# A four-layer graph network: the second product of layer 1 as seven block products, and sums that may stand on either of two engines

## The chip, the core and the metric

The kernel runs on one core of one Trainium2 chip. The core has five engines that run side by side, each with its own queue of instructions in a fixed order: TensorE (PE: matrix products, with PEld for its weight loads), VectorE (DVE), ScalarE (ACT), GpSimd (POOL) and SyncE (SP, which issues transfers). They share the on-chip memory SBUF; products land in PSUM, eight banks of 128 x 512 numbers. An instruction waits until what it needs is there, and everything behind it on its engine waits too.

The metric is the device time of one execution, in microseconds (us).

## What is computed

Input are 128 graphs of 64 nodes with 256 features, float32 throughout, and their adjacency matrices. Four layers follow each other, each as x = layernorm(x + layer(x)):

```python
# layer 0: five steps of a gated update
m = h @ weight[l];  agg = adj^T @ m
r, z = sigmoid(i_r + h_r), sigmoid(i_z + h_z);  n = tanh(i_n + r * h_n)
h = (1 - z) * n + z * h                 # i from agg @ w_ih.T, h_* from h @ w_hh.T
# layer 1
agg = epsilon * x + adjacency @ x
h = silu(rmsnorm(agg @ W1 + b1) * rms_weight)       # 1024 wide
out = h @ W2 + b2                                    # back to 256
# layer 2: log map, adj @ x, exponential map, projection onto the ball
# layer 3: attention with weights exp(e_i + f_j) masked by adj
```

The change is mostly about `h @ W2` in layer 1: per group of graphs a product of 512 x 1024 by 1024 x 256.

## The kernel before

Two graphs make one block of 128 nodes, so that an adjacency block is 128 x 128 with two filled quarters. Four blocks make a group (`NB` = 4, `R` = 512 nodes), and there are 16 groups. `group(g)` (called once per group) records every operation of one group for all four layers; nothing is run while it records. Operations go to one engine (`pe`, `dve`, `act`, `pool`) or are recorded with two possible ones (`flow.either`, used by `copied` and `scaled` for ScalarE or VectorE), each with an assumed duration.

`Flow.issue` then lays the order of all engines. It is a planner, `Plan.advance`: it keeps a clock per engine, looks at the next operations of up to four groups at a time (`WINDOW`), and takes the one that can begin first by the assumed durations; ties are broken by a rank. The rank is one of a few rules (earliest group first, latest group first, or longest remaining path with a lag per group), and `CHOICES` holds a digit for every stretch of `STRETCH` us that says which rule holds there. The string was found by a search. The order so found is fixed: each instruction is tied behind its predecessor on the engine, and only the real waits decide when it runs. Operations flagged `port` are kept from overlapping between VectorE and GpSimd in the plan.

Buffers: a group's tiles live in one of three slots (`s = g % 3`), under tags (`A`, `B`, `U`, `V`, `agg`, `h`, `y`, `hs`, `adjT`); a new tile under a tag waits until all users of the one before are done. The 4-wide tiles of the norms (`tiny`) have two buffers for each name and slot.

The places that matter here, by line of the profile:
- L745 to L749: sums and differences of halves of h or agg, which feed the gates' products. These, and layer 1's first product (L949), are already seven block products in place of eight.
- L762 and L768: the gates' products. Both take 256 columns at a time.
- `state_side`: two quarters of intermediate results in the tile `hs` (L773, L788).
- L884 to L887: the last three steps of the gated update on VectorE.
- L933 and L343: squares of the 1024 hidden features on ScalarE, and their sums (GpSimd, on VectorE in the last two groups). L343 is the helper `pool_sum`, also used to add the biases b2 (`xb`) and W_b (`x_n`).
- L998 and L1000: scaling by the root mean square (VectorE), then silu (ScalarE), for 8 chunks of 128 features. L991, L692 and L1062 are powers of 4 or 8 numbers on GpSimd.
- L313 with `ps_o`: the product with `w2s`, the whole of W2 in SBUF. For every block of 128 nodes 8 chunks of 128 features are multiplied by 256 columns and accumulated:

```python
for k in range(KH):
    pe(256, lambda ps=ps, b=b, j=j, k=k: matmul(
        ps[:, j * D:(j + 1) * D], chunk(k)[0][:, b * P:(b + 1) * P], w2s[:, k, :], k, KH),
        [ps], [*chunk(k)[1], (w2s, k)])
```

- L667, `onto_rows`: the result is added onto the residual on VectorE; in all but the last two groups the same instruction also gives the row's sum for the norm.
- `layer_norm`: the row's sum to a mean (L679), sum of squares on ScalarE (L681), the power on GpSimd (L692), and the scaling (L336 or L337). The last two groups use VectorE's own row statistics (L688, L689).
- L313 also stands for other products (`matmul`): `ps_agg` (aggregation, 128 columns at a time), `ps_sup`, `ps_a`, `ps_att` of layers 2 and 3.

Of the kernel before, what the change touches and what calls it, by code (L numbers as in the profile page):

```python
# [13 lines left out]
AF = mybir.ActivationFunctionType  # L14
# [39 lines left out]
class Plan:  # L54
# [15 lines left out]
    def advance(self, until, rank):  # L70
# [3 lines left out]
        while self.left and clock["PE"] < until:  # L74
            best = None
            for s in range(self.first, min(self.first + flow.WINDOW, len(self.queues))):
                for e, q in self.queues[s].items():
                    opened = False
                    for _, o in zip(range(flow.AHEAD[e]), q):
# [12 lines left out]
                        key = (t + flow.SOONER if len(o.ways) > 1 and e == "DVE" else t, *rank(s, o))  # L92
# [36 lines left out]
class Flow:  # L129
# [16 lines left out]
    SOONER = 0.4  # L146
# [6 lines left out]
    WINDOW, STRETCH, LAGS = 4, 6.0, (0.0, 60.0, 150.0)  # L153
    CHOICES = ("0010000320333333330030000000030000303010330000003330300030300030300003033330301303000001103313000330"
               "0001000001010301301300133000000000300003030301031033030033000000031033031033030300303333030330010330"
               "0000330000300333303103003030300300030130000033000303030000333301300103300003300000003301000033003033"
               "3000000111310003100100311030000003300111101111202220010111101102112122201121121202122111000")
# [81 lines left out]
def kernel(  # L239
# [50 lines left out]
    small = ctx.enter_context(tc.tile_pool(name="small", bufs=2))  # L290
# [51 lines left out]
    def pool_sum(n, o, x0, x1, w, r):  # L342
        pool(0.24 + 0.00211 * n, lambda: nc.gpsimd.tensor_tensor(o(), x0(), x1(), OP.add), w, r)  # L343
# [85 lines left out]
    vecs = unit("hs", S, "vecs", (P, 2, P))  # L429
# [128 lines left out]
    w2s = fixed([P, KH, D], "w2s")  # L558
    flow.op("SP", 0.6, lambda: nc.sync.dma_start(w2s.tile(), w2.rearrange("(k p) d -> p k d", p=P)), [w2s], kb=1024)
# [41 lines left out]
    def group(g):  # L601
# [14 lines left out]
        def tiny(name, shape=(P, NB), dt=F32):  # L616
            t = f"{name}{s}"
            return Buf(lambda: small.tile(list(shape), dt, tag=t, name=f"{name}_{g}"), slot=(t, 2))
# [53 lines left out]
        def layer_norm(y, st, tag, name, norm=None):  # L672
# [4 lines left out]
            m = 2 if norm else 1  # L677
            if summed:
                dve(4, lambda: nc.vector.tensor_scalar(mv[:, :, 0], st[:, :, 0], -1.0 / D, None, OP.mult), [mv], [st])  # L679
                for b in range(NB):  # L680
                    act(400, lambda b=b: nc.scalar.activation(  # L681
                        o[:, b, :], y[:, b, :], AF.Square, bias=mv[:, b, 0:1], accum_out=st[:, b, 1:2]),
                        [(o, b), (st, (1, b))], [(y, b), mv])
                dve(8, lambda: nc.vector.scalar_tensor_tensor(  # L684
                    ve[:, :m, :], over(st[:, :, 1], m), 1.0 / D, eps2[:, :m, :NB], OP.mult, OP.add), [ve], [st])
            else:
                for b in range(NB):
                    dve(256, lambda b=b: nc.vector.bn_stats(st[:, b, :], y[:, b, :]), [(st, b)], [(y, b)])  # L688
# [9 lines left out]
            for b in range(NB):  # L698
                scaled(256, lambda b=b: o[:, b, :], lambda b=b: y[:, b, :], lambda b=b: rstd[:, 0, b:b + 1],
                       lambda b=b: off[:, b:b + 1], [(o, b)], [(y, b), off, rstd], ("DVE",))  # L700
# [21 lines left out]
        def gated(l, h):  # L722
# [20 lines left out]
            def sums(x, i):  # L743
                t = t_of[i]
                dve(R, lambda: nc.vector.tensor_sub(t[:, :2, :], x[:, :, half(1)], halves_of(x[:, 0, :])),  # L745
                    [(t, t1), (t, t3)], [x], True)
                dve(HR, lambda: nc.vector.tensor_sub(t[:, t2, :], x[:, 1, half(1)], t[:, t1, :]),
                    [(t, t2)], [(x, 1), (t, t1)], True)
                dve(HR, lambda: nc.vector.tensor_sub(t[:, t4, :], t[:, t2, :], x[:, 1, half(0)]),  # L749
                    [(t, t4)], [(x, 0), (t, t2)], True)  # L750
# [24 lines left out]
            def state_side():  # L775

                px, py = bank("p_hx"), bank("p_hy")
                hs = u("hs", f"hs{l}", (P, 2, HR))
                su, sv = ((lambda i=i: hs[:, i, :]) for i in range(2))
# [12 lines left out]
                copied(HR, su, lambda: px[:, :HR], [(hs, 0)], [px])  # L792
# [3 lines left out]
                onto(su, px, 1, su, [(hs, 0)], [(hs, 0)])  # L796
                prod(py, 0, w_hn, ms3, sum_of(t3)[1], True)
                onto(sv, py, 0, su, [(hs, 1)], [(hs, 0)])
                prod(py, 1, w_hn, ms1, sum_of(t1)[1])
                prod(py, 0, w_hn, mn22, sum_of(t4)[1])  # L800
                biased(0, 1, py, 0, su, (hs, 0))
                biased(1, 1, py, 1, sv, (hs, 1))
                prod(py, 1, w_hn, ms4, block(1, 1)[1])
                biased(1, 0, py, 1, su, (hs, 0))
# [354 lines left out]
```

## Time and profile before

| what | value |
|---|---|
| median of 3 runs | 2367.19 us (2366.66 to 2367.27) |
| the profiled execution, its time | 2366.68 us |
| its span from first to last instruction | 2364.9 us |
| instructions in the span | 32771 |
| matmul instructions | 11986 |
| read from and written to device memory | 24.69 MB, 8.39 MB |
| granted TensorE clock, mean | 0.994 |

How to read it: the span is cut into busy time per engine; a group of the profile is all instructions of one line, engine, operation and tile, with its count, the time it covers, the mean length of one, and the idle time of the engine just before them with who ended it. The chain of waits goes back from the last instruction to what released each step. A float32 matmul of the code appears as two instructions, each with its own weight load.

### The profile page before, as it was taken

How to read it: one execution, taken by the hardware profiler on the slowest of the kernel's cores; microseconds unless marked ns; L12 is line 12 of the kernel's file. 1: busy time of each engine (PE TensorE's matmuls, PEld its weight loads, DVE VectorE, ACT ScalarE, POOL GpSimd, SP SyncE). 2: the span in 40 equal slices, each digit the busy share in tenths (PEclk: the TensorE clock that was granted, in tenths of full speed). 3: DMA queues.
4: the chain of work that ended last, by engine and by line, in shares of the span. 5: the costliest groups of instructions: out<-in, count | busy, mean ns of one | idle time of the engine just before them, and what ended most of it. 6: DMA issues, size and time to landing. Idle time of an engine off the chain costs nothing.

```text
span 2364.9 us, 32771 instructions
## 1 busy us (share of the span) xinstructions
PE 2329.6 (99%) x11986; PEld 2046.1 (87%) x11986; DVE 1904.2 (81%) x4271; ACT 1236.0 (52%) x2643; POOL 340.1 (14%) x272
## 2 busy tenths in 40 slices
PE   9999999999999999999999999999999999999996
PEld 7888888888888888888888888888888888888874
DVE  5788887887878778787887878787787887788986
ACT  3334555555555555555555555455554555444375
POOL 3102111021010212102021110212102020001021
PEclk9999999999999999999999999999999999999997
DMA  3000000000000000000000000000000000000000
GB/s 123 10 1 12 1 30 1 21 9 1 30 1 27 3 1 30 1 30 1 18 12 1 30 1 27 3 1 30 1 30 1 10 21 1 19 10 1 19 1 27
DMA packets 39440, 35.17 MB, mean 15 GB/s; under 512 B 9924, under 2 KB 38624, under 8 KB 39280
## 3 DMA queue, kind: packets, MB, share of 16 engines
q1 hardware_dynamic: 37552, 31.20, 4.2%
q8 instruction: 95, 1.56, 0.3%
q10 hardware_dynamic: 1328, 1.31, 0.2%
q0 software_dynamic: 400, 0.57, 0.1%
q14 instruction: 65, 0.53, 0.1%
HBM read 24.69 MB, written 8.39 MB: 14 GB/s over the span
## 4 chain that ended last, share of the span: by engine, by line
PE 91%; DVE 7%; ACT 1%; issue 1%; POOL 0%; POOLq 0%; ACTq 0%; DVEq 0%
PE p_r L762 11%; PE p_w L762 11%; PE p_v L762 11%; PE ps_o L313 9%; PE ps_agg L313 7%; PE p_hy L768 6%; PE p_u L762 6%; PE p_iy L768 5%; PE p_hx L768 4%; PE p_ix L768 4%; PE ps_hr L644 3%; PE ps_a L313 2%; PE p_vh L949 2%; PE p_wh L949 2%; PE p_1h L949 2%; PE ps_sup L313 1%
## 5 line engine op out<-in xcount | busy, mean ns | idle before, releaser
L692 POOL TENSOR_TENSOR rstd<-ve,pow 128x4 f32<-128x4 f32 (+1 forms) x64 | 77.7, 1214 | 1319.4 <-DVE ve L684 1213.9
L313 PE MATMUL ps_o<-w2s,hid 128*128 128x256 f32 x1024 | 229.8, 380 | 0.9 <-ACT hid L1000 0.9
L313 PEld LDWEIGHTS ps_o<-w2s,hid 128*128 128x128 f32 x1024 | 193.1, 190 | 28.6 <-ACT hid L1000 2.8
L762 PE MATMUL p_v<-tA,w_h 128*128 128x256 f32 x640 | 170.5, 380 | 0.0
L762 PE MATMUL p_r<-hT,w_h 128*128 128x256 f32 x640 | 168.6, 380 | 1.6 <-DVE U L813 1.2
L762 PE MATMUL p_v<-tB,w_a 128*128 128x256 f32 x640 | 169.8, 379 | 0.0
L762 PE MATMUL p_r<-agg,w_a 128*128 128x256 f32 x640 | 167.7, 379 | 0.0
L816 ACT ACTIVATE U<-U,half_b 128x512 f32<-128x512 f32 (+1 forms) x160 | 94.1, 628 | 107.7 <-DVE U L813 107.4
L313 PEld LDWEIGHTS ps_agg<-edge,hr 128*128 128x128 f32 x1024 | 138.3, 191 | 8.2 <-ACT hr L331 0.2
L313 PE MATMUL ps_agg<-edge,hr 128*128 128x128 f32 x1024 | 140.0, 275 | 0.0
L788 DVE SCALAR_TENSOR_TENSOR hnb<-p_hy,half_b,hs 128x256 f32<-128x256 f32 x240 | 108.8, 479 | 37.1 <-PE p_hy L768 36.3
L331 ACT COPY agg<-ps_agg 128x512 f32<-128x512 f32 x145 | 84.4, 584 | 99.1 <-PE ps_agg L313 98.5
L762 PEld LDWEIGHTS p_v<-tB,w_a 128*128 128x128 f32 x640 | 120.5, 190 | 15.8
L768 PE MATMUL p_hy<-tA,w_hn 128*128 128x256 f32 x480 | 131.8, 380 | 2.1 <-DVE hs L773 0.8
L762 PEld LDWEIGHTS p_r<-agg,w_a 128*128 128x128 f32 x640 | 119.6, 190 | 15.3
L768 PE MATMUL p_iy<-tB,w_in 128*128 128x256 f32 x480 | 132.4, 379 | 0.0
L762 PEld LDWEIGHTS p_v<-tA,w_h 128*128 128x128 f32 x640 | 118.6, 190 | 15.2 <-DVE U L813 0.4
L331 ACT COPY hr<-ps_hr 128x512 f32<-128x512 f32 x117 | 67.9, 583 | 121.7 <-PE ps_hr L644 120.7
L762 PEld LDWEIGHTS p_r<-hT,w_h 128*128 128x128 f32 x640 | 115.0, 190 | 15.1 <-DVE U L813 1.6
L816 ACT ACTIVATE V<-V,half_b 128x256 f32<-128x256 f32 (+1 forms) x160 | 86.3, 584 | 77.6 <-DVE V L813 77.5
L681 ACT ACTIVATE x_n<-y,mv 128x256 f32<-128x256 f32 x168 | 83.3, 497 | 81.9 <-DVE mv L679 81.8
L1000 ACT ACTIVATE hid<-hid,cols 128x512 f32<-128x512 f32 x128 | 85.9, 716 | 76.6 <-DVE hid L998 76.5
(259 smaller groups left out, 5844.6 us busy)
## 6 DMA issues: line engine op xcount, KB each, us to landing
x<-in_x_dram SPq DMA_DIRECT2D x16, 512.0 KB, 3.4
xr<-in_x_dram SPq DMA_DIRECT2D x16, 512.0 KB, 3.5
out_dram<-x_n SPq DMA_DIRECT2D x16, 512.0 KB, 2.9
edge<-in_adj_dram SPq DMA_DIRECT2D x32, 64.0 KB, 2.3
wm<-in_L_gnn_weight_dram SPq DMA_DIRECT2D x5, 256.0 KB, 4.8
w2s<-in_L_gnn_W_dram SPq DMA_DIRECT2D x1, 1024.0 KB, 9.3
w_in_L_gnn_w_hh_dram<-in_L_gnn_w_hh_dram ACTq DMA_DIRECT2D x1, 512.0 KB, 5.2
w_in_L_gnn_w_ih_dram<-in_L_gnn_w_ih_dram ACTq DMA_DIRECT2D x1, 512.0 KB, 6.9
```

Source lines behind the costliest of these rows:

```text
L313: return nc.tensor.matmul(o, lhsT, rhs, start=(k == 0), stop=(k == nk - 1))
L331: flow.either([("ACT", 0.22 + 0.00077 * n, lambda: nc.scalar.copy(o(), i())), ("DVE", 0.145 + 0.00105 * n, lambda: nc.vector.tensor_copy(o ...
L644: turn(lambda j=j, c=c: nc.tensor.transpose(ps[:, j * D + c * P:j * D + (c + 1) * P], src[:, c, (HB * n + j) * P:(HB * n + j + 1) * P], id ...
L681: act(400, lambda b=b: nc.scalar.activation(o[:, b, :], y[:, b, :], AF.Square, bias=mv[:, b, 0:1], accum_out=st[:, b, 1:2]), [(o, b), (st, ...
L692: pool(1.25, lambda: nc.gpsimd.tensor_tensor(rstd[:, :m, :], ve[:, :m, :], pow2[:, :m, :NB], OP.pow), [rstd], [ve])
L762: pe(HR, lambda i=i, w=w, c=c: nc.tensor.matmul(ps[:, c * HR:(c + 1) * HR], w[:, m, c * P:(c + 1) * P], v[i][0](), start=first and i == 1 ...
L768: pe(HR, lambda: nc.tensor.matmul(ps[:, j * HR:(j + 1) * HR], w[:, m, :], v[0](), start=first, stop=True, skip_group_check=True), [ps], [( ...
L788: dve(HR + 44, lambda: nc.vector.scalar_tensor_tensor(out(n, c)(), ps[:, j * HR:(j + 1) * HR], b(c), x(), OP.add, OP.add), [(hnb, (n, c))] ...
L816: act(HR if len(w) == 1 else R, lambda: nc.scalar.activation(o(), src(), AF.Tanh, bias=half_b[:, i * KD + c:i * KD + c + 1], scale=0.5), w ...
L949: pe(HR, lambda c=c: nc.tensor.matmul(ps[:, c * HR:(c + 1) * HR], w1f[:, w, (2 * q + c) * P:(2 * q + c + 1) * P], v[0](), start=first and ...
L1000: act(R, lambda v=v, c=c: nc.scalar.activation(v, v, AF.Silu, scale=rmsc(c)), parts, [*parts, cols], SILU)
```

## The change

Layer 1's second product goes by blocks. The activations are cut into two halves of nodes by two halves of features (a11, a12, a21, a22), W2 into two halves of features by two halves of columns. Seven products of [256 x 512] by [512 x 128] replace eight; four sums of weight blocks are made once at the start on GpSimd, four sums of activation blocks per group (each in two parts, 512 numbers a partition). A product's result is added onto the residual `y1` directly, in quarters; the product with wd2 belongs to three quarters. Since the quarters no longer end with whole rows, the row sums of that norm come from a pass of ScalarE (`of` in `layer_norm`).

Sums of two SBUF tiles (`summing`) may now stand on VectorE or GpSimd; the planner takes the one that can begin first, with a handicap of 1.5 us for GpSimd (`LATER`). This covers L745 to L749, L884, the sums of squares, the biases, the differences of layer 1's first product and the new sums. In layers 2 and 3 several 4-wide tiles share names, and each has one buffer instead of two. `hs` is gone: its quarters lie in `uz`. The tile for every second square, `sqh`, is one for all groups. The order of the scalings L998 is changed to (0, 1, 4, 5, 2, 3, 6, 7). The rules and the string `CHOICES` are new, with stretches of 4 us.

```diff
-                        key = (t + flow.SOONER if len(o.ways) > 1 and e == "DVE" else t, *rank(s, o))
+                        key = (t + flow.LATER.get((e, len(o.ways) > 1 and o.eng), 0.0), *rank(s, o))
...
-    SOONER = 0.4
+    LATER = {("DVE", "ACT"): 0.4, ("POOL", "DVE"): 1.5}
...
-    WINDOW, STRETCH, LAGS = 4, 6.0, (0.0, 60.0, 150.0)
+    WINDOW, STRETCH, LAGS = 4, 4.0, (60.0,)
...
-    small = ctx.enter_context(tc.tile_pool(name="small", bufs=2))
+    small = ctx.enter_context(tc.tile_pool(name="small", bufs=1))
...
-    def pool_sum(n, o, x0, x1, w, r):
-        pool(0.24 + 0.00211 * n, lambda: nc.gpsimd.tensor_tensor(o(), x0(), x1(), OP.add), w, r)
+    def summing(n, o, x0, x1, op, w, r):
+
+        def run(v):
+            return lambda: v.tensor_tensor(o(), x0(), x1(), op)
+        flow.either([("DVE", 0.145 + 0.00105 * n, run(nc.vector)), ("POOL", 0.24 + 0.00211 * n, run(nc.gpsimd))], w, r, port=("DVE", "POOL"))
...
-    w2s = fixed([P, KH, D], "w2s")
-    flow.op("SP", 0.6, lambda: nc.sync.dma_start(w2s.tile(), w2.rearrange("(k p) d -> p k d", p=P)), [w2s], kb=1024)
+    w11, w21, w22, wd1, wd2, wd3, wd4 = range(7)
+    KQ = KH // 2
+    w2k = w2.rearrange("(i k p) (n d) -> i n p k d", i=2, p=P, n=2)
+    w2f = fixed([P, 7, KQ, P], "w2f")
+    for o, k, n in ((w11, 0, 0), (w21, 1, 0), (w22, 1, 1), (wd3, 0, 1)):
+        flow.op("SP", 0.6, lambda o=o, k=k, n=n: nc.sync.dma_start(w2f[:, o], w2k[k, n]), [(w2f, o)], kb=256)
+    for o, x0, x1 in ((wd1, wd3, w11), (wd2, w22, wd1), (wd3, w22, wd3), (wd4, w21, wd2)):
+        pool(1.3, lambda o=o, x0=x0, x1=x1: nc.gpsimd.tensor_tensor(w2f[:, o], w2f[:, x0], w2f[:, x1], OP.subtract),
+             [(w2f, o)], [(w2f, x0), (w2f, x1)])
...
-            return Buf(lambda: small.tile(list(shape), dt, tag=t, name=f"{name}_{g}"), slot=(t, 2))
+            return Buf(lambda: small.tile(list(shape), dt, tag=t, name=f"{name}_{g}"), slot=(t, 1))
...
+            if summed and of:
+                for b in range(NB):
+                    act(400, lambda b=b: nc.scalar.activation(
+                        o[:, b, :], y[:, b, :], AF.Identity, accum_out=st[:, b, 0:1]), [(o, b), (st, (0, b))], row(b))
...
-                hs = u("hs", f"hs{l}", (P, 2, HR))
-                su, sv = ((lambda i=i: hs[:, i, :]) for i in range(2))
+                su, sv = ((lambda c=c: uz[:, c, half(0)]) for c in range(2))
...
-        for c in range(KH):
+        for c in (0, 1, 4, 5, 2, 3, 6, 7):
...
-        for h in range(2):
-            ps = bank("ps_o1")
...
+        def by_sums_back():
+            px, py = bank("p_ox"), bank("p_oy")
+            a11, a21, a12, a22 = ([block(i + q, n) for q in range(2)] for i in (0, 2) for n in range(2))
...
+            s1, s2, s4 = other("agg", "s1"), other("V", "s2"), other("U", "s4")
+
+            def sums(q):
+                for o, x0, x1, op in ((s1, a21, a22, OP.add), (s2, s1, a11, OP.subtract), (a21, a11, a21, OP.subtract), (s4, a12, s2, OP.subtract)):
+                    summing(R, lambda o=o: val(o[q]), lambda x0=x0: val(x0[q]), lambda x1=x1: val(x1[q]), op,
+                            o[q][1], [*x0[q][1], *x1[q][1]])
+
+            def prod(ps, i, w, v, first=False):
+                for j in range(HB):
+                    for k in range(KQ):
+                        pe(128, lambda j=j, k=k: nc.tensor.matmul(
+                            ps[:, i * HR + j * P:i * HR + (j + 1) * P], val(v[k // 2])[:, k % 2, j * P:(j + 1) * P], w2f[:, w, k, :],
+                            start=first and j == 0 and k == 0, stop=j == HB - 1 and k == KQ - 1, skip_group_check=True),
+                            [ps], [(w2f, w), *v[k // 2][1]])
...
+            prod(px, 0, w11, a11, True)
+            prod(px, 1, w21, a12)
+            onto(0, 0, px, 0)
+            onto(0, 0, px, 1)
+            prod(py, 0, wd3, a21, True)
+            prod(py, 1, wd1, s1)
+            onto(1, 1, py, 0)
+            onto(1, 1, py, 1)
+            prod(px, 0, wd2, s2)
+            onto(0, 1, px, 0)
+            dve(2 * HR + 20, lambda: nc.vector.tensor_add(
...
+            prod(py, 0, wd4, a22)
+            prod(py, 1, w22, s4)
+            onto(1, 0, py, 0)
+            onto(0, 1, py, 1)
```

## The prediction

> **What bounds the kernel now.** I read the busy table first, then the stretches, then the chain of waits, then the groups of instructions with their shapes.
>
> The busy table of the page, and busy time by stretch (columns: stretch, its length, then busy time and count of TensorE matmuls, TensorE weight loads, VectorE, ScalarE, GpSimd, then the granted clock, the share of the DMA engines and GB/s):
>
> ```profile
> PE 2329.6 (99%) x11986; PEld 2046.1 (87%) x11986; DVE 1904.2 (81%) x4271; ACT 1236.0 (52%) x2643; POOL 340.1 (14%) x272
> ```
>
> ```profile
> 0.00:60.00 60.00, 57.45 (x277) 44.80 (x278) 32.32 (x90) 20.13 (x50) 18.77 (x36) 1.00 0.38 122
> ...
> 900.00:1200.00 300.00, 299.26 (x1551) 263.67 (x1550) 246.77 (x551) 165.22 (x356) 45.40 (x33) 1.00 0.05 14
> ...
> 2240.00:2312.00 72.00, 66.32 (x330) 56.27 (x330) 62.67 (x169) 49.92 (x101) 14.54 (x10) 1.00 0.00 1
> 2312.00:2365.00 53.00, 32.21 (x119) 23.53 (x117) 33.89 (x139) 30.49 (x83) 10.98 (x9) 0.73 0.09 30
> ```
>
> The matmul row is idle for 2364.9 - 2329.6 = 35.3 us in all: 2.6 in the first 60 us, 5.7 from 2240 to 2312, 20.8 in the last 53, which leaves 6.2 for the 2180 us between. So through the steady part time is the sum of what TensorE streams, and in the tail it is the latency of the last groups. Busy time of a pipelined engine is not its price, so I take the price from the chain of waits (start, length, what), where runs of one shape stand alone, and check the instruction counts in the groups:
>
> ```profile
> 817.18 13.81 PE ps_o L313 x64
> 1340.17 1.78 PE ps_agg L313 x16
> ```
>
> ```profile
> L313 PE MATMUL ps_o<-w2s,hid 128*128 128x256 f32 x1024 | 229.8, 380 | 0.9 <-ACT hid L1000 0.9
> L313 PEld LDWEIGHTS ps_o<-w2s,hid 128*128 128x128 f32 x1024 | 193.1, 190 | 28.6 <-ACT hid L1000 2.8
> L313 PE MATMUL ps_agg<-edge,hr 128*128 128x128 f32 x1024 | 140.0, 275 | 0.0
> ```
>
> A 256-wide matmul instruction takes 13.81/64 = 0.2158 us of the stream; a 128-wide one, each with weights of its own, takes 1.78/16 = 0.1113. (Each fp32 matmul of the code is two instructions in the trace.) The mean durations of 380 and 275 ns overlap each other and are not prices.
>
> VectorE is the second engine, and GpSimd can hold it up. The rows to see are one sum of two SBUF tiles on each engine, and a 4-element VectorE step that took 2.07 us, from 2318.42, while GpSimd ran a sum of 2.35 us from 2318.11:
>
> ```profile
> L745 DVE TENSOR_TENSOR tA<-hT 128x512 f32<-128x512 f32 x80 | 57.4, 717 | 7.6 <-ACT hT L331 5.9
> L343 POOL TENSOR_TENSOR sqt<-sqt,sqh 128x512 f32<-128x512 f32 x56 | 74.2, 1325 | 152.0 <-ACT sqh L933 148.7
> ```
>
> ```profile
> 2318.42 2.07 DVE L1024 SCALAR_TENSOR_TENSOR fac<-n,fac 128x4 f32<-128x4 f32 x1
> ```
>
> **What the Trainium skill says.** "TensorE: Matmul & The Clock Gate", section "Back-to-back issue gap": in a stream of weight loads and matmuls both set the spacing, so narrow matmuls gain less than their width. The trace agrees mildly: half the width costs 0.1113/0.2158 = 0.516, not 0.5. The same page, "What's actually happening": an idle TensorE falls to half its clock. The granted clock of 0.73 in the last 53 us agrees. "GPSIMD Engine Reference", section "8. Key points": GpSimd shares its SBUF interfaces with VectorE, and contends with VectorE instructions that have two SBUF inputs. The 2.07 us step above agrees.
>
> **The change part by part**, against the profiled execution (span 2364.9 us).
>
> *Products.* Out go 16 groups x 4 row blocks x 8 chunks = 512 matmuls, 1024 instructions: 1024 x 0.2158 = 221.0 us. In come 16 x 7 products x 2 row blocks x 4 chunks = 896 matmuls of 128 columns, 1792 instructions: 1792 x 0.1113 = 199.5. Removed: 21.5 us, 1.34 per group. All other TensorE instructions keep count and shape. The new ones look like ps_agg (128x128 weights, 128 columns moving). Bounds of the pitch: 0.1079 (half of 0.2158) would make it 27.6 us; 0.1233 is where nothing is gained. The ps_agg run excludes that for a stream of 16, so I keep 0.1113.
>
> *VectorE.* Per-instruction times are from the groups; counts are from the order of both programs' instructions.
> - Goes: 64 adds of ps_o onto xb with their accumulator reads, 24.4 + 4.6 = 29.0 us.
> - Comes: 112 adds of a 256-wide product part at 0.42 (as L833's 256-wide rows, 421 to 424 ns) = 47.0; 16 of 512 at 0.69 = 11.0.
> - Comes: of the 128 new block sums (512 wide) 82 stand on VectorE, 82 x 0.69 = 56.6; 46 go to GpSimd.
> - Moves from GpSimd: 92 additions of squares, 63.5; 15 of xb and 11 of x_n (1024 wide, 1.23), 32.0.
> - Moves to GpSimd: 32 of h - n, 11 and 28 of tA and tB, one of ts, 512 wide, 72 x 0.69 = 49.7; 67 of 256 at 0.42 = 28.1.
> - Copies and scalings between VectorE and ScalarE: -17.7 net (11 agg, 3 aggm, 5 hs, 10 hnb and 8 tan leave, 7 of x_n come).
> Sum +85.6: VectorE goes from 1904 to about 1990 us, 85% of a span near 2350. It costs nothing as long as TensorE's stream covers it.
>
> *GpSimd.* 92 x 1.27 + 26 x 2.36 = 178 us leave. 72 + 46 sums of 512 at 1.27, 67 of 256 at 0.73 (L417's w_a at 26.38) and four weight sums come, 204. About 366 us: the time in which it can hold VectorE up is nearly what it was. Its powers of the norms (L692, L991, L1062) now queue behind other people's sums, up to 1.27 us each.
>
> *ScalarE.* 56 row sums (Identity with accumulator) at 0.52 each, 29 us; 16 us of the copies above; 3 table loads more (48 for 45), 3.8. 1236 becomes about 1285, 55%. Covered.
>
> *Loads, buffers.* w2s as one transfer of 1 MB becomes four of 256 KB, three more issues on SP ahead of the third group's x and edge. That x is due near 46 us and the weights near 200, so I take 0 (0 to 2). Small tiles get one buffer for two: a norm's 4-wide tiles wait for the previous norm of the same group, which lies a layer back, so 0. The tile hs goes; its two quarters now live in uz, which is the tag of the previous step's uu, so the state side's first copy waits for that step's last VectorE operation. Other groups' matmuls are ready meanwhile; I count it with the stalls.
>
> *Stalls in the steady part.* 6.2 us of matmul idle with VectorE free 19% of the time. Free 15% afterwards, scaled, gives 8; and the adds and sums now fall into the burst that used to let VectorE catch up (in the 14 us of the burst at 817 it was busy 5.0). I take +4 us in all; bounds 0 and +20 (1.25 us per group).
>
> *Tail.* Before, three groups are still in layers 2 and 3 after the last product (2313 to 2356 in the timeline: 16 instructions of ps_sup, 48 of ps_a, 24 of ps_att, 24 transposes). In the new order only the last two are, side by side, after their products. The chain of the last group is what it was: 51.5 us from the last ps_o (2313.4) to the end. It loses the 1.9 us of the blocked step and some queueing behind a third group; it gains two more row statistics (1.1) and a table load and ScalarE copies of the other group ahead of its Ln and Tanh (about 4). I keep 51. TensorE had 88 x 0.216 + 24 x 0.11 = 21.6 us of work for that stretch and has 16 + 32 + 16 instructions and 16 transposes now, 15.6; the missing 6 stand earlier, where they are paid in full. (0.11 is the chain's ps_rms, 4 in 0.44 us.) So +6 us (bounds 0 and +10).
>
> Sum: -21.5 + 4 + 6 = -11.5; span 2353.4. The profiled execution before took 2366.7 in all and the median is 2367.2, 2.3 above its span: 2355.7, rounded to 2355.
>
> **Rivals.**
> - *A, stalls eat the gain* (no change). VectorE and GpSimd at the new load stall TensorE by another 0.7 us per group: +11, time 2366. For it: 85%, and one order for three busy engines. Against it: 6.2 us of idle in 2180 now.
> - *B, slower.* VectorE becomes the bound at the new product. A product burst of 12.5 us of TensorE brings VectorE 8 x 0.74 of scaling (L998), 5 x 0.69 of sums and 3.6 us of adds, 13 us, where before it brought 5.9 + 1.8; if a group's burst finds VectorE already late (from 676 to 692 us it was busy 15.1 of 16), each wait is paid by TensorE. It decides from 1.0 us of extra stall per group ((21.5 - 6)/16); at 2.2 us per group, two fifths of the 5.3 us of work added there, 35 us go and the time is 2367.2 - 15.5 + 35 = 2387.
> - *C, the full gain.* The tail is no longer (the third group's work fits elsewhere, the chain shrinks by what queued behind that group) and stalls stay at 6: 2367.2 - 21.5 = 2346.
>
> **How the numbers follow.** Forecast 0.64, C 0.14, A 0.12, B 0.10. The forecast's own range is 2350 to 2362; with C and the near half of A it is 2345 to 2366, which leaves out about 0.2. Within 0.2% (4.7 us, about what a measurement here tells from no change) of 2367.2 is 2362.5 to 2371.9: it gets A and a little of the forecast's edge, less A's outer part, 0.12; slower is B with that part, 0.11; faster 0.77.
>
> **What would show it.** Products: 1792 instructions of p_ox and p_oy, runs in the chain at 0.111 per instruction. Load: VectorE near 1990 us, GpSimd 366, ScalarE 1285. Stalls: matmul idle between 60 and 2200 us of 6 to 14 us. Tail: matmul idle in the last 55 us of about 26. The forecast is wrong if that steady idle is over 20 us, or if waits of TensorE on s, hid or on the adds onto xb come to more than a microsecond per group.

## The result, and the profile after

| | before | after |
|---|---|---|
| median of 4 runs each, us | 2366.93 | 2378.09 |
| lowest to highest, us | 2365.20 to 2367.27 | 2377.02 to 2379.42 |
| span of the profiled execution, us | 2364.9 | 2375.1 |
| TensorE idle from 60 to 2240 us | 6.3 | 19.7 |
| TensorE idle from 2240 us to the end | 26.4 | 36.0 |

The ratio is 1.0049, with a 95% interval from 1.0032 to 1.0066: the change makes the kernel half a per cent slower, where 11.5 us of gain were forecast. Below, "idle" is always a stretch's length less the busy time of its matmuls.

The busy table after:

```profile
PE 2317.0 (98%) x12754; PEld 2056.6 (87%) x12754; DVE 1988.6 (84%) x4305; ACT 1272.5 (54%) x2793; POOL 378.6 (16%) x343
```

VectorE was forecast at about 1990 us, GpSimd at 366, ScalarE at 1285: the load was read rightly. A line of the chain of waits has the price of the new product, 3.57/32 = 0.1116 us per instruction, so that 1792 of them take 200.0 us for the 221.0 of the old ones:

```profile
2311.65 3.57 PE p_oy L1042 x32
```

Busy time by stretch after (columns as in the prediction: stretch, length, TensorE matmuls, weight loads, VectorE, ScalarE, GpSimd, granted clock, DMA share, GB/s):

```profile
60.00:2240.00 2180.00, 2160.29 (x11942) 1927.91 (x11941) 1846.53 (x3897) 1165.95 (x2560) 316.52 (x275) 1.00 0.04 12
900.00:1200.00 300.00, 295.63 (x1648) 263.74 (x1647) 257.47 (x568) 172.57 (x390) 39.30 (x34) 1.00 0.06 18
2240.00:2312.00 72.00, 61.07 (x323) 52.14 (x322) 65.51 (x152) 53.49 (x111) 30.64 (x23) 0.91 0.02 8
2312.00:2375.00 63.00, 38.08 (x217) 31.74 (x216) 41.65 (x166) 32.02 (x74) 11.72 (x9) 0.80 0.08 26
```

The reader is to see three things. From 900 to 1200 us TensorE is idle 4.4 us where it was 0.7. From 2240 to 2312 it is idle 10.9 us where it was 5.7, and its clock is 0.91 there where it was 1.00. And the matmul row as a whole fell by 12.7 us (2329.6 to 2317.0) although the product gave 21.0: some 8 us of loss stand inside what counts as busy, as matmuls that follow each other more slowly.

What TensorE waits for, after, then three rows of before (columns: total us, times, longest us):

```profile
PE ps_sup L315 <- ACT tan L1110: 10.8, 3, 9.5
PE ps_hr L656 <- DVE hT L907: 6.5, 8, 1.3
PE ps_T L646 <- ACT x_n L338: 5.4, 3, 2.6
PE p_vh L967 <- DVE hid L972: 4.9, 3, 2.9
...
PE p_hy L788 <- DVE V L793: 2.3, 3, 1.0
PE p_hy L788 <- DVE hnb L807: 2.0, 3, 1.4
PE p_ix L788 <- DVE V L852: 1.7, 3, 1.2
PE p_iy L788 <- DVE V L852: 1.4, 2, 1.1
```

```profile
PE p_r L762 <- DVE U L813: 1.2, 1, 1.2
...
PE p_hy L768 <- DVE hnb L788: 0.6, 1, 0.6
...
PE ps_hr L644 <- DVE hT L887: 0.5, 1, 0.5
```

The first row after is almost all in the tail (one wait of 9.5 us). The rows that grew are hT, hnb, V and U, all of them results of the recurrent cells of layer 0; before, they came to a few single waits. There is no row of p_ox or p_oy: the product that was changed isn't where TensorE waits.

One such wait, followed back. VectorE's timeline (start, length, engine, line, what), then GpSimd's, then the wait of TensorE in brackets:

```profile
1027.79 0.69 DVE L347 TENSOR_TENSOR hT<-hT,V 128x512 f32<-128x512 f32 x1 [0.34 <-ACT V L899]
1028.52 1.65 DVE L905 SCALAR_TENSOR_TENSOR hT<-U,hT 128x512 f32<-128x512 f32 x1
1030.20 0.69 DVE L907 SCALAR_TENSOR_TENSOR hT<-hT,V 128x512 f32<-128x512 f32 x1
...
1033.85 1.13 DVE L699 TENSOR_SCALAR mv<-st 128x4 f32<-128x4 f32 x1
1034.90 0.68 DVE L905 SCALAR_TENSOR_TENSOR hT<-U,hT 128x512 f32<-128x512 f32 x1
1035.61 0.69 DVE L907 SCALAR_TENSOR_TENSOR hT<-hT,V 128x512 f32<-128x512 f32 x1
```

```profile
1027.89 1.73 POOL L347 TENSOR_TENSOR hT<-hT,V 128x512 f32<-128x512 f32 x1 [7.47 <-ACT V L899]
1033.69 1.27 POOL L347 TENSOR_TENSOR tB<-agg 128x512 f32<-128x512 f32 x1 [4.07 <-ACT agg L333]
```

```profile
1036.45 0.41 PE L656 MATMUL ps_hr<-ident,hT 128*128 128x128 f32 x2 [1.30 <-DVE hT L907]
```

L905 takes 0.68 us at 1034.90, but 1.65 at 1028.52, where GpSimd's half of the same hT runs until 1029.62. L699, on four columns, takes 1.13 us because GpSimd's tB runs from 1033.69 to 1034.96. VectorE has no pause between the two, so both delays are passed on through its queue to L907 at 1035.61, and TensorE waits 1.30 us for it. A hold here is such a lengthening. The Trainium skill has it under "SBUF — State Buffer", section "SBUF: two separate sides": whichever of the two starts first gets the port pair that VectorE and GpSimd share for its whole instruction, and the other blocks fully. This trace agrees: VectorE's own half of hT began first and took its usual 0.69 us, GpSimd's half took 1.73 where tB took 1.27, and L905 behind them ended 0.55 us after GpSimd did.

I followed every wait of TensorE of over 0.2 us between 60 and 2240 us back through 8 us of its chain in the same way. After, 24 of 28 such waits (16.7 of 19.2 us) have in their chain a VectorE instruction that took over 0.1 us longer than the median of its form while a GpSimd operation ran; before, 9 of 10 (5.9 of 6.1 us). No GpSimd sum stands in these chains after the change as a link itself. That is an association; the runs below test it.

Which instructions were lengthened, by the same mark of 0.1 us, from 60 to 2240 us? Before, they add up to 36 us, 32 of them on results of the cells (hT, tA, tB, U, V) and none on the four-wide steps of the norms. After, it is 49 us: 26 on results of the cells and 16 on four-wide steps, these beside GpSimd's tB and hT above all. So the results of the cells were held before as well, and somewhat more; what is new is the four-wide steps. They carry no `port` flag, so the plan didn't keep them apart from GpSimd.

### The profile page after: what moved, and what is told of

It reads as the page before. It is cut to its first block, busy times and chain, and to the rows that moved or that the text cites. A ratio compares the mean times of both kernels' runs of the same rounds, so it can differ in the third digit from the quotient of the medians.

```text
span 2375.1 us, 34664 instructions
## 1 busy us (share of the span) xinstructions
PE 2317.0 (98%) x12754; PEld 2056.6 (87%) x12754; DVE 1988.6 (84%) x4305; ACT 1272.5 (54%) x2793; POOL 378.6 (16%) x343
## 3 DMA queue, kind: packets, MB, share of 16 engines
q8 instruction: 101, 1.65, 0.3%
## 4 chain that ended last, share of the span: by engine, by line
PE 88%; DVE 9%; ACT 2%; issue 1%; POOL 1%; POOLq 0%; ACTq 0%; DVEq 0%
PE p_w L782 11%; PE p_v L782 11%; PE p_r L782 11%; PE ps_agg L315 7%; PE p_hy L788 6%; PE p_iy L788 5%; PE p_u L782 5%; PE p_oy L1042 5%; PE p_hx L788 4%; PE p_ix L788 4%; PE p_ox L1042 4%; PE ps_hr L656 3%; PE p_vh L967 2%; PE p_1h L967 2%; PE p_wh L967 2%; PE ps_a L315 2%
## 5 line engine op out<-in xcount | busy, mean ns | idle before, releaser
L333 ACT COPY agg<-ps_agg 128x512 f32<-128x512 f32 x156 | 91.1, 584 | 121.8 <-PE ps_agg L315 121.1
L899 ACT ACTIVATE V<-V,cols 128x512 f32<-128x512 f32 x96 | 64.7, 715 | 104.0 <-DVE V L852 103.9
L338 ACT ACTIVATE x_n<-y,off,rstd 128x256 f32<-128x256 f32 x175 | 92.3, 589 | 46.3 <-DVE off L716 46.2
L656 PE MATMUL ps_hr<-ident,hT 128*128 128x128 f32 x640 | 101.4, 273 | 6.8 <-DVE hT L907 6.5
L656 PEld LDWEIGHTS ps_hr<-ident,hT 128*128 128x128 f32 x640 | 79.7, 141 | 25.9 <-issue 9.9
```

Of the source, the lines that this page charges most:

```text
L333: flow.either([("ACT", 0.22 + 0.00077 * n, lambda: nc.scalar.copy(o(), i())), ("DVE", 0.145 + 0.00105 * n, lambda: nc.vector.tensor_copy(o ...
L338: flow.either([("ACT", 0.3 + 0.0008 * n, lambda: nc.scalar.activation(o(), i(), AF.Identity, bias=bias(), scale=scale())), ("DVE", 0.145 + ...
L656: turn(lambda j=j, c=c: nc.tensor.transpose(ps[:, j * D + c * P:j * D + (c + 1) * P], src[:, c, (HB * n + j) * P:(HB * n + j + 1) * P], id ...
L899: act(R, lambda c=c: nc.scalar.activation(uu[:, c, :], uu[:, c, :], AF.Tanh, bias=bih(2 * KD + c)), [*of(uu, 0, c), *of(uu, 1, c)], [*of(u ...
```

## The experiments

Theories named in the expectations: T1, GpSimd's sums hold VectorE and TensorE waits for what comes late (T1b: those of the new product do the harm); T2, VectorE's higher load does it; T3, the planned order has too little slack whoever does the sums; T5, the shared small tiles; K, TensorE's own waits lower its clock in the run-in (2200 us to the last product). All runs, each with its ratio to the kernel before on the same chip; runs on different chips are best compared by this ratio:

| run | median us | ratio, 95% interval | idle 60 to 2240 | VectorE | GpSimd |
|---|---|---|---|---|---|
| after | 2378.09 | 1.0049 [1.0032, 1.0066] | 19.7 | 1988.6 | 378.6 |
| e1_sums_vector | 2400.67 | 1.0148 [1.0133, 1.0163] | 24.8 | 2033.8 | 145.3 |
| e2_sums_scalar | 2368.28 | 1.0009 [1.0002, 1.0016] | 11.3 | 1942.8 | 144.9 |
| e3_blocksums_scalar | 2384.96 | 1.0086 [1.0069, 1.0103] | 22.2 | 1938.4 | 373.5 |
| e5_before_sums_vector | 2375.07 | 1.0039 [1.0024, 1.0054] | 10.7 | 1955.2 | 138.6 |
| e7_blocksums_gpsimd_away | 2383.15 | 1.0071 [1.0054, 1.0088] | 20.2 | 1985.4 | 315.5 |
| e8_gru_sums_away | 2369.03 | 1.0014 [1.0007, 1.0021] | 13.4 | 1952.7 | 228.1 |
| e9_before_shared_small | 2365.88 | 1.0001 [0.9992, 1.0009] | 6.9 | 1903.2 | 339.9 |
| v1_after_reordered_holds | 2394.03 | 1.0118 [1.0104, 1.0132] | 28.4 | 1907.7 | 810.5 |
| c1_after_reordered_blind | 2423.17 | 1.0242 [1.0228, 1.0256] | 47.4 | 1927.5 | 848.0 |
| b1_before_reordered_holds | 2378.11 | 1.0050 [1.0037, 1.0064] | 21.3 | 1958.4 | 339.2 |
| g1_fifteen_back | 2381.60 | 1.0066 [1.0054, 1.0079] | 21.7 | 1987.4 | 361.3 |
| g2_fifteen_others_back | 2378.49 | 1.0053 [1.0040, 1.0066] | 18.9 | 1992.9 | 359.5 |
| h1_fifty_moves | 2377.41 | 1.0046 [1.0032, 1.0060] | 20.9 | 1987.3 | 364.7 |
| k1_after_filled_waits | 2374.83 | 1.0041 [1.0028, 1.0053] | 19.7 | 1987.9 | 378.4 |
| k2_before_filled_waits | 2364.40 | 0.9994 [0.9986, 1.0002] | 6.3 | 1903.1 | 340.1 |

### GpSimd's sums to VectorE, or away altogether

The first diff is e1's, the second e2's, both where the planned order is issued:

```diff
+            if eng == "POOL" and "DVE" in o.ways:
+                eng = "DVE"
             made = o.ways[eng][1]()
```

```diff
+            if eng == "POOL" and o.alt:
+                eng, run = "ACT", o.alt
+            else:
+                run = o.ways[eng][1]
-            made = o.ways[eng][1]()
+            made = run()
...
+        flow.ops[-1].alt = lambda: nc.scalar.copy(o(), x0())
```

> The changed kernel in its own order, but every one of GpSimd's 195 sums is issued on VectorE at the same place of the order; GpSimd keeps its powers and its 4 weight differences. Theory T1 (GpSimd's sums hold VectorE's instructions at the SBUF port, and TensorE then waits for what VectorE brings late): although VectorE's busy time rises from 1988.6 to about 2040-2060 us, TensorE's idle time between 60 and 2240 us falls from 19.7 us to under 15, and the time from 2378 to 2372 or less. T2 (VectorE's load itself makes its results late): the idle time stays or grows, 19 to 40 us, time 2378 to 2400. T3 (the planned order leaves too little slack whoever does the sums): within 3 us of 2378.

> The changed kernel in its own order, but each of GpSimd's 195 sums is replaced by a ScalarE copy of its first operand, so the second operand is left out of the result there (values of the output differ). GpSimd is left with its powers and 4 weight differences, ScalarE gets about 110 us more, VectorE keeps its instructions. T1: TensorE's idle time between 60 and 2240 us falls from 19.7 to about 10, time about 2366-2370. T2: VectorE has the same instructions, only those it was held in get shorter; idle falls by a third at most, time 2372-2378. T3: no change, 2375-2381.

e1 gave T2's figures in idle time and, within a microsecond, in time. Its waits are others, though: TensorE now waits for the sums themselves, which stand in VectorE's queue at places that were chosen for GpSimd, and hT has nearly gone (1.2 us in all). Idle time also understates e1: of its 26 us of added span 16 are in busy time, as matmuls that follow each other more slowly.

```profile
PE p_v L784 <- DVE tB L349: 7.0, 17, 0.8
...
PE p_u L784 <- DVE tB L349: 4.8, 8, 1.4
```

e2 fell between T1 and T2 in idle time (11.3 us) and met T1 in time. Its waits in the steady part:

```profile
PE p_u L787 <- ACT tB L353: 3.9, 8, 1.2
PE p_v L787 <- ACT tB L353: 3.2, 6, 0.6
```

These 7.1 us are for the substitute copies on ScalarE; if they are simply subtracted, 4.2 us of idle time are left, less than the 6.3 of the kernel before (an estimate: no run has neither the sums nor the copies). The waits for hT and hnb are gone. T3 thus doesn't hold for the steady part: the order is the same. For the run-in it stays open, see below. No chain of e1 or e2 holds a lengthened VectorE instruction.

e2 also measures the holds. VectorE has the same instructions as after and is busy 1942.8 instead of 1988.6 us: 195 sums on GpSimd lengthened its instructions by 45.8 us, 0.23 us per sum. One group of them, after and then in e2 (line, engine, what, count, busy us, mean ns, idle before):

```profile
L905 DVE SCALAR_TENSOR_TENSOR hT<-U,hT 128x512 f32<-128x512 f32 x96 | 74.1, 772 | 2.1
```

```profile
L910 DVE SCALAR_TENSOR_TENSOR hT<-U,hT 128x512 f32<-128x512 f32 x96 | 66.5, 693 | 3.3 <-ACT hT L353 1.2
```

The same sums on VectorE itself (e1) take 2033.8 - 1942.8 = 91.0 us, 0.47 each. So on average a sum on GpSimd costs VectorE half of what it costs there, but at a moment that nobody chose.

### Which sums: the product's own, or the cells'

As e2, but only sums that carry a mark are replaced. e3 and e7 mark the product's s1, s2, a21 and s4, e8 marks tA, tB and hT of the cells; e3 replaces those that VectorE makes (first diff), e7 and e8 those that GpSimd makes (second):

```diff
+            if eng == "DVE" and o.back:
...
                     summing(R, lambda o=o: val(o[q]), lambda x0=x0: val(x0[q]), lambda x1=x1: val(x1[q]), op,
                             o[q][1], [*x0[q][1], *x1[q][1]])
+                    flow.ops[-1].back = True
```

```diff
+            if eng == "POOL" and o.back:
```

> The changed kernel in its own order, but the 82 sums of the second product that VectorE makes (s1, s2, a21, s4) are replaced by ScalarE copies of their first operand, so the second operand is left out there (values of the output differ); GpSimd keeps all its 195 sums. VectorE falls from 1988.6 to about 1930 us. T1: idle of TensorE from 60 to 2240 us stays at 17-20 us, time within 2 us of 2378. T2: it falls to about 12 or less, time 2366-2371. T3: no change.

> The changed kernel in its own order, but only the 46 sums of the second product's blocks that GpSimd makes (s and hid, 63.3 us of its busy time) become ScalarE copies of their first operand (the second operand is left out there, values of the output differ); GpSimd keeps its other 149 sums. After the first four runs theory T1 stands as: GpSimd's sums hold VectorE, and the ones that do harm are those that fall beside hT, hnb, tan and the four-wide operations. T1 in this form: most of the 9.8 us that taking all sums away brought does not come; TensorE's idle time from 60 to 2240 us 15 to 20 us, time 2373-2378. Rival T1b (the new product's own sums do the harm): idle falls to about 11 us, time about 2368.

> The complement of the run before in its call: only the 136 sums of the recurrent cells that the search put on GpSimd (tA, tB, hT, about 150 us of its busy time) become ScalarE copies of their first operand (the second operand is left out there, values of the output differ); the 46 block sums stay on GpSimd. T1: most of the gain comes, idle 10 to 14 us, time 2367-2371; the placement by the search, not the product, is then what costs. T1b: idle 17 to 20 us, time 2374-2378.

In e3, 50 us less of VectorE's time left the steady stalls where they were (22.2 us). So T2 isn't the cause in the sense of the prediction, in which the new product's own work makes VectorE late. The time even rose by 7 us, beyond what T1 had forecast; 3.5 us of it are waits of the product for the substitute copies on ScalarE (p_oy), the rest wasn't traced. In e7 the steady part didn't move either (20.2), which speaks against T1b, and hT is still there:

```profile
PE ps_hr L661 <- DVE hT L912: 6.5, 8, 1.3
```

The 46 sums of e7 hardly held VectorE: without them it is busy 3.2 us less, without e8's 136 it is 35.9. (e7's median is 5 us above the changed kernel's, 5 more than T1 allowed; by the ratios the intervals overlap.)

e8 brings 8 us by the ratio and 9.1 by the medians, most of e2's gain, and hT leaves the list. Its runs lie from 2366.6 to 2372.3 us, and the profiled one, 2371.7, is among the slowest, so that its trace shows less of the gain than the median. Of its 13.4 us of idle time 6.9 are again for the substitute copies:

```profile
PE p_u L789 <- ACT tB L353: 3.7, 8, 1.2
PE p_v L789 <- ACT tB L353: 3.2, 6, 0.6
```

Subtracted, that leaves 6.5, the 6.3 of the kernel before. The steady loss comes with the 136 sums of the recurrent cells that the search put on GpSimd, not with waits of the new product. That doesn't acquit the product altogether: these sums have to stand somewhere, and on VectorE, with the product's sums beside them, they cost more (e1). The new product with the placement of the kernel before wasn't run. What is shown is the effect of taking these sums away; that the holds, and not the sums' own length on GpSimd, carry it rests on the chains: they have lengthened VectorE instructions in 24 of 28 waits after and in 4 of 19 in e8. No run separates holds on results of the cells from holds on four-wide steps.

### One part of the change, or the load, on the kernel before

e9 (first diff) and e5 (second):

```diff
-    small = ctx.enter_context(tc.tile_pool(name="small", bufs=2))
+    small = ctx.enter_context(tc.tile_pool(name="small", bufs=1))
...
-        ms, rms = tiny("ms"), tiny("rms")
+        ms, rms = tiny("rn"), tiny("fac")
...
-        rd = tiny("rd")
+        rd = tiny("ser")
```

```diff
+            if o.alt:
+                eng, run = "DVE", o.alt
...
+        flow.ops[-1].alt = lambda: nc.vector.tensor_tensor(o(), x0(), x1(), OP.add)
```

> The kernel before with the third part of the change alone: small tiles with one buffer each instead of two, and ms, rms and rd in the tiles of rn, fac and ser; its order stays. Theory T5 (the shared small tiles make four-wide operations wait for readers of the tile's last use): slower than 2366 by 2 us or more. If the small tiles are free: within 1.5 us of the kernel before.

> The kernel before in its own order, but GpSimd's 128 sums (98 of sqt, 16 of xb, 14 of x_n) are issued on VectorE at the same place of the order: VectorE from 1904 to about 1990 us, the changed kernel's load, and hardly a GpSimd sum left to hold it. T1: TensorE's idle time between 60 and 2240 us stays at 6.2 us or falls, time 2362-2368. T2: it grows toward the changed kernel's 19.7 us, time 2372-2385. T3: 2366-2370.

The small tiles are free. The other changes of buffers and of the scalings' order weren't run alone. e5 is a surprise for T1 and gives the time that T2 forecast: with hardly a sum on GpSimd the kernel before gets 9 us slower, and its idle time grows from 6.3 to 10.7. VectorE's own time in these places isn't free either. So sums on GpSimd aren't bad as such: in the kernel before, where they were mostly those of the squares in layer 1 (98 of 128), they were better placed there than on VectorE.

### Can an order that knows the holds repair it?

For v1, c1, b1 and h1 another order was searched in a replay: the plan's operations with the plan's own durations, in a given order, where operations wait for each other as the code has it and, except in c1, VectorE operations that read SBUF alone also for GpSimd's sums. g1 only moves sums that the replay accuses. v1, c1 and b1 issue a whole order that is written out; h1 makes 51 moves (first diff), g1 and g2 change the engine of 15 sums (second):

```diff
+        for at, to, eng in self.MOVES:
+            plan.order.insert(to, (eng, plan.order.pop(at)[1]))
```

```diff
-        for eng, o in plan.order:
+        for at, (eng, o) in enumerate(plan.order):
+            if at in self.BACK:
+                eng = "DVE"
```

> The changed kernel with another order of its instructions and another choice of engine for its sums and copies, found by a local search (moves of one instruction, changes of one engine) from the changed kernel's own order; for the search every VectorE operation that reads SBUF alone, the four-wide ones too, waits while a GpSimd sum runs, and the reverse. Every value is computed as before. T1 (what the plan did not know are the holds, and they are the steady stalls): TensorE's idle time from 60 to 2240 us falls from 19.7 to 8 us or less, and the time to 2345-2360, below the kernel before. T2 (VectorE's load): the order can't help much, 2368 or more. T3 (any order is too tight on the chip, whatever the plan knows): 2365-2380.

> Control for the run before it in this call: the same local search from the same order with as many seconds, but with only the operations flagged in the changed kernel's own plan waiting for GpSimd's sums; the four-wide and 64-partition ones don't. T1: the search fills GpSimd (768 operations in place of 337) without seeing what it holds, so that TensorE's idle time from 60 to 2240 us grows beyond the 19.7 us of the changed kernel, to 30-60 us, time 2390-2420. If it was the search alone that helps (T3's reverse): as fast as the run before it, within 4 us.

> The kernel before with the same local search, from its own order, with the holds known; its sums stay on the engines that they have, only copies change engines. It sets the two products beside each other under orders found in one way. If the new product is worth its 20.6 us of TensorE time once the order suits it: this run is 6 to 14 us slower than the changed kernel so reordered, 2352-2366. If the gain of the product is eaten in any order: within 3 us of it or faster.

Searched without knowledge of the holds, the order was 29 us slower than searched with it (one search each), which speaks for holds that matter to an order. But v1 missed its mark by more than 30 us and lies outside every forecast. It more than doubled GpSimd's time, and although VectorE's busy time fell to 1907.7 us, the kernel before's level, its idle steady time is 28.4 us: VectorE's busy share doesn't tell how long TensorE waits. b1 shows why no product can be judged by these runs: the same search made the kernel before slower too, though it stays 16 us ahead of v1. The replay's durations are averages; that an order fitted to them has no slack for the rest is the likely reason, but wasn't tested.

> The changed kernel in its own order, but 15 of GpSimd's 195 sums are issued on VectorE at their place in the order: those for which a replay of the order, in which VectorE operations that read SBUF alone wait for GpSimd's sums, says that they delay TensorE (7 of tB<-agg with 512 columns, 3 of hT, 5 small ones; one of them is the sum at 704 us beside which the five multiply-adds of line 1099 took 2.35 us). Every value is computed as before. T1 (few holds at the wrong places make the stalls): 4 to 8 us faster than the changed kernel, 2370-2374, idle time of TensorE from 60 to 2240 us from 19.7 to about 13, although VectorE gets about 9 us of sums more. T2 (load) or T3 (a tight order): not faster, 2376-2382.

> Control for the run before it in this call: as many of GpSimd's sums of the same kinds (15, 7 of them tB<-agg with 512 columns), but drawn at random from those that the replay doesn't accuse, are issued on VectorE at their place. T1: no gain, 2377-2382, idle 19 to 22 us. If fewer sums on GpSimd help wherever they are: as fast as the run before it.

> The changed kernel with 51 changes of its order found in the same replay, each taken only if it brings 0.15 us there: 16 sums from GpSimd to VectorE and 3 the other way, 3 other changes of engine, and 29 instructions a few places earlier or later (8 to 9 of TensorE's, some in the last 100 us). Every value is computed as before. T1: the steady stalls nearly go, idle of TensorE from 60 to 2240 us 5 to 10 us, and 2358-2368 in all, no slower than the kernel before. If single moves are overfitted to the replay, as the free search was (2394): 2370 or more.

T1 in the form "a few sums at the wrong places" has fallen: g1 isn't faster than the changed kernel, nor than its control. Waits for tB took the place of some, and hT stayed; in two waits a GpSimd sum is now the releaser itself:

```profile
PE ps_hr L662 <- DVE hT L913: 6.5, 7, 1.3
...
PE p_v L788 <- DVE tB L353: 2.8, 5, 1.2
PE p_u L788 <- DVE tB L353: 2.7, 2, 2.1
PE p_u L788 <- POOL tB L353: 2.3, 2, 1.5
```

The arithmetic of e1 and e2 fits that: a sum moved to VectorE saves a hold (0.23 us on average) and puts its own time (0.47) in the same queue. h1 is no better (2377.41, where T1 forecast 2358 to 2368). No order tried here lets the new product beat the kernel before.

### The clock in the run-in

Pieces of the chain of waits after (start, length, what):

```profile
2248.83 1.00 DVE n L1085
2249.85 1.21 DVE fac L1087
...
2266.90 2.07 PE p_vh L967 x4
...
2276.79 0.86 PE p_vh L967 x4
...
2300.20 5.86 PE p_ox L1042 x30
...
2315.22 3.13 PE p_ox L1042 x28
```

Four instructions of p_vh take 2.07 us at 2266.90 and 0.86 at 2276.79; 30 of p_ox take 5.86 at 2300.20, where 28 take 3.13 later. The granted clock is 0.50 from 2264.2 to 2270.8 us and from 2298.4 to 2305.0, 1.00 from 2271 to 2298, and it was 1.00 from 2240 to 2312 before. The first two lines are four-wide steps of another group's norm, held (their usual length is 0.16), ahead of hid in VectorE's queue.

The fillers, issued ahead of the matmul that waits:

```diff
+    def fill(n):
+        ps = psum.tile([P, 512], F32, tag="bank", name="fill")
+        return [nc.tensor.matmul(ps[:, :D], ident_t, w1f[:, 0, :D], start=True, stop=True) for _ in range(n)]
```

> The changed kernel, and in nine of TensorE's waits after 2240 us extra matmuls of 256 columns (47 in all, about 0.43 us each at the full clock, fewer than the wait holds) into a bank of their own that nothing reads; they add work and change no value. In the changed kernel the granted clock falls to half twice ahead of the last product (p_vh x4 took 2.07 us for 0.86, the first 30 of p_ox 5.86 for 3.35, some 5.6 us in all) and again in the tail. Theory K (TensorE's own waits in the run-in lower its clock, and that is half of what the run-in lost): the clock stays at 1.00 and the run-in and the tail give back 4 to 10 us, 2368-2374. Rival (the clock falls for another reason, or the fillers get in the way): 2377-2382.

> The kernel before with the same kind of fillers in nine of its waits after 2240 us (31 matmuls of 256 columns, about 0.43 us each). Its clock falls only from 2334 us on, in the tail. Theory K: the tail's matmuls go at the full clock, 2358-2364, faster than both kernels. Rival: 2365-2369.

Windows of k1, in which the fillers count as matmuls, and its p_vh:

```profile
2240.00:2312.00 72.00, 67.39 (x372) 57.62 (x371) 66.45 (x155) 54.41 (x112) 30.60 (x23) 0.98 0.04 14
2312.00:2372.30 60.30, 45.71 (x262) 39.02 (x261) 40.33 (x164) 31.11 (x72) 11.69 (x9) 0.90 0.06 20
```

```profile
2267.90 0.86 PE p_vh L972 x4
```

With the waits filled the clock goes from 0.91 to 0.98 up to 2312 us and from 0.80 to 0.90 after it, and the p_vh that took 2.07 us takes 0.86. So the lowered clock is a consequence of TensorE's waits. What k1 brings is less than K forecast: the last product ends 1.4 us earlier (2326.70 for 2328.15), the span is 2.7 us shorter, the median of 2374.83 lies between the ranges of both theories, and the ratio's interval overlaps that of the changed kernel. k2 is the kernel before within its interval. The waits that the fillers fill remain, and a filler can hold up the matmul behind it; k1's clock also still falls to 0.50 from 2298.6 to 2301.8 us. So what a full clock alone would be worth isn't shown.

## Why the prediction was wrong

Its steps in turn, with what they measured:

- *Products, -21.5.* Right: 0.1116 us per instruction, -21.0.
- *Load of the engines, cost 0.* The sizes were right within 13 us each. That the cover holds was wrong, see the next step.
- *Stalls in the steady part, +4, bounds 0 and +20.* This is the step that failed first. Idle time grew by 13.4 us, and counted from start to start of the matmuls against their usual spacing, which takes in gaps too short to be listed, by about 16.1. The step scaled 6.2 us by VectorE's free share. It had dismissed GpSimd in one sentence, "the time in which it can hold VectorE up is nearly what it was". GpSimd's time was indeed near the forecast (378.6 us for 366), but equal time isn't equal harm: VectorE's lengthened instructions add up to 49 us for 36, with the four-wide steps of the norms newly among them, and the 136 sums of the recurrent cells, which weren't on GpSimd before, cost some 8 to 9 us by e8.
- *Tail, +6.* The last group's chain was kept at 51 us; it measures 2375.1 - 2328.15 = 46.9. The 6 us of the third group's work moved ahead of it as foreseen. So +1.4 instead of +6.
- *What had no step.* This is a failure of the same size. Between 2200 us and the last product TensorE lost some 12 us more against its work than before (about 20 for 8). The prediction looked at 2313 us and later only. The waits of over 0.25 us there come to 10.5 us, 5.7 before; the rest is mostly matmuls at a lowered clock, which k1 could only partly win back. The holds aren't the main cause there: e2, without any of these sums on GpSimd, keeps 17.8 us of lost time from 2200 to 2300 us (17.6 after). Nor is it this one order: by the same count every run with the new product loses 17 to 27 us there (11 with fillers), v1's and c1's orders included, and every run of the kernel before 4 to 8, b1's included. Which dependence sets these waits wasn't isolated, so the cause of this half stays open.

Together: -21.0 + 16.1 + 1.4 + 12.2 = +8.7, of the +10.1 us of span; 1.4 us are left unassigned, about what the count depends on the spacing that it takes as usual. (The prediction's own sum, 2355.7, was rounded to 2355 where it should have been 2356; nothing hangs on it.)

Rival B forecast "slower", which came true, with a mechanism that didn't: bursts of the new product. There is no wait of p_ox or p_oy, and e3 took 50 us of that work off VectorE without effect. Rival A (2366) had the size of the steady stalls, 11 us more, but not the rest. Its mechanism, VectorE and GpSimd stalling TensorE at the new load, is the nearest to what was found. Of the signs named, steady idle time (19.2 us from 60 to 2200) came up to the limit of 20 without passing it, so the limit was set too wide to notice the loss; the waits on hid, 8 us in all, stayed under a microsecond per group, and none on s or the adds onto xb is listed.

## What to carry to other kernels

When work is moved to GpSimd, ask not only how long GpSimd is busy but which VectorE instructions stand beside it, the small ones too, and what TensorE needs next from them: here nearly the same GpSimd time went with 6 us of stalls in one kernel and with 20 in the other. A change that gives TensorE back time is worth that time only where TensorE is the bound: price the run-in as well as the tail, and every stage whose slack the freed time was. And of the four orders fitted to a replay here (v1, c1, b1, h1) none kept on the chip what it gained on paper: keep the order that has been measured as the one to beat.

## What the runs showed of the hardware

- A hold hits more than sums of two tensors. L699 and L735 have one tensor operand in SBUF; L699, on four columns, took 1.13 us in the lines above, where its usual length is 0.17. No instruction that reads a PSUM tile was lengthened: of L832's 400 instructions of 512 columns about 80 ran beside a GpSimd operation, of L1016's 128 it was 84, and none took over 0.1 us more than the median.
- The hold goes both ways, and the one that begins first isn't slowed. In the lines above a GpSimd sum of 512 columns took 1.27 us for tB, and 1.73 for hT, which began 0.10 us after VectorE's sum of the other half of the same tile; that sum took 0.69 us, its usual length.
- Useless matmuls in TensorE's waits kept its clock up (0.91 to 0.98 in the run-in). The p_vh above started 1.0 us later for them (2267.90 for 2266.90) and still ended 0.2 us earlier.
